# Last sequence of an attention and mixture-of-experts block: residual sums on VectorE, counts added behind the rank, half of the one-hots on GpSimd

## The chip, the cores and the metric

One core of a Trainium2 chip runs one launch of the kernel. The time is device microseconds of that launch, the median of several runs. Instruction times come from one profiled execution, in microseconds from the start of its span. The engines are TensorE (PE, with its weight loads as PEld), VectorE (DVE), ScalarE (ACT), GpSimd (POOL) and SyncE (SP, which here only issues DMAs).

## The reference, cut to what matters

Eight sequences of 256 tokens of width 256 go through an attention layer (16 query heads, 4 key and value heads of 128) and a mixture-of-experts layer (8 experts, two per token, and one shared expert). Both have a normalisation ahead and behind and a residual sum.

```python
x = x + _layernorm(attn(_layernorm(x)))
x = x + _layernorm(ffn(_layernorm(x)))

# ffn, on xf = all 2048 tokens
logits = xf @ gate_w.T
weights, indices = top_k(softmax(logits), 2)      # weights then divided by their sum
out = sum over the 2 experts of weight * (silu(xf @ w_gate[e]) * (xf @ w_up[e])) @ w_down[e]
out = out + sigmoid(xf @ shgate_w) * (silu(xf @ shw_gate) * (xf @ shw_up)) @ shw_down
```

## The kernel before, in words

The 2048 tokens are 16 tiles of 128 tokens, two per sequence: tile i is sequence b = i // 2, half t = i % 2. The last sequence, b = 7, owns tiles 14 and 15.

The order of the work is written out by hand: inside `tc.manual_schedule()` each engine runs its instructions in the order in which the program names them. An engine never passes an instruction that waits, so whatever stands behind it on that engine waits as well. A loop over steps `s` lays the projections, the attention and the routing of several sequences beside each other, each helper with a delay of its own. What does not fit into the loop stands behind it, line by line, for sequence `z = B - 1`.

For each tile the helpers that matter here are, in their order:

- `output` multiplies the attention result by the output weights (L638, PE, into PSUM tile `o`).
- `residual` takes mean and variance of `o` on DVE (`norm_stats`, L258 to L261: `st_o`, `mv_o`), and raises the variance plus epsilon to -0.5 on POOL (L262, `rstd_o`).
- `residual_sum` normalises `o` into `y` on DVE (`norm_apply`, L267) and adds `y` to the residual stream `x_all` on POOL (L653).
- `inner` takes the statistics of `x_all` (again L258 to L262: `st_f`, `mv_f`, `rstd_f`), `inner_rows` normalises into `xf` on DVE (L267) and sends the rows to memory through SP's queue (L663).
- `turn_inner` transposes `xf` on PE (L671, `tf`), ACT copies it into `xfT` (L672).
- `route` computes the router's logits on PE (L678, `r`) and picks the two experts on DVE (L687 to L703); `chosen` and its sum `ch` are one-hots over the 8 experts.
- `rank` counts, on PE, how many earlier tokens took the same expert (L724, L725, `rank`). On DVE, `at` adds an offset (L727), `count` adds this tile's choices to running counts in bf16 (L729, over 64 elements for the first tiles down to 8 for the last), and `pk`, `place`, `pu`, `pr` and `rc` (L733 to L745) turn the rank into a row and a column.
- `mark` writes, for each of the two experts k, three one-hots of 128x128 in bf16 on DVE into one tile `hot` (L756, L757, L761); that tile has one buffer.
- `enter` multiplies the one-hots on PE (L772, `in`): four products per tile, (k = 0, n = 1), (0, 2), (1, 1), (1, 2), each with `hot[k, 0]` as weights. DVE adds the result to `member` (L776).

`fill(n)` puts parts of the shared expert between them: `gus` (L285, PE), `sl` (L297, ACT), `hT` (L298, DVE), `sd` (L305, PE), and a scaled copy (L312, ACT).

Behind the last sequence, `table` sums the counts on PE (L1035, `total`), and a chain on DVE (L1039 to L1060), with PE in between (L1065, L1072), gives the list of tokens of each block. POOL fetches the blocks' rows by indirect DMA (L1136), and 39 blocks follow, each with transposes, two multiplications by the weights of its expert, and a store (L1146 to L1197). At the end the rows are gathered again, combined, normalised and stored.

The order behind the loop, for the last sequence (cut to the calls on the tiles' way):

```python
            for o in range(H, 2 * H):
                output(z, o)
            inner(z, 0)
            inner_rows(z, 0)
            fill(2)
            turn_inner(z, 0)
            residual(z, 1)
            route(z, 0)
            residual_sum(z, 1)
            fill(1)
            rank(z, 0)
            inner(z, 1)
            mark(z, 0)
            inner_rows(z, 1)
```

Of the kernel before, what the change touches and what calls it, by code (L numbers as in the profile page):

```python
# [15 lines left out]
ALU = mybir.AluOpType  # L16
# [3 lines left out]
P = 128  # L20
B, S, HID = 8, 256, 256
# [7 lines left out]
E, TOPK, HE, HS = 8, 2, 176, 352  # L29
# [11 lines left out]
G = len(ENDS)  # L41
# [7 lines left out]
def block_kernel(  # L49
# [18 lines left out]
    nc = tc.nc  # L68
# [10 lines left out]
    x_all = const.tile([P, NTILES, HID], F32, name="x_all")  # L79
# [62 lines left out]
    for j, w in enumerate((wg, wu)):  # L142
# [42 lines left out]
    count = const.tile([P, G, E], BF16, name="count")  # L185
# [14 lines left out]
    iota_p = const.tile([P, P], BF16, name="iota_p")  # L200
    nc.gpsimd.iota(
        iota_p, pattern=[[1, P]], base=0, channel_multiplier=0,
# [49 lines left out]
    stats = {}  # L252
# [12 lines left out]
    def norm_apply(dst, src, name):  # L265
        mean, rstd = stats.pop(name)
        nc.vector.tensor_scalar(dst, src, mean, rstd, ALU.subtract, ALU.mult)  # L267
# [97 lines left out]
    with ExitStack() as actx:  # L365
# [16 lines left out]
        now = {}  # L382
# [266 lines left out]
        def residual_sum(b, t):  # L649
            i = b * NT + t  # L650
            y = xw.tile([P, HID], F32, tag="y", name=f"y_{i}")
            norm_apply(y, now.pop(("o", b, t)), f"o_{i}")
            nc.gpsimd.tensor_tensor(x_all[:, i, :], x_all[:, i, :], y, ALU.add)  # L653

        def inner(b, t):
            i = b * NT + t
# [63 lines left out]
        def rank(b, t):  # L720
            i = b * NT + t
            ch = now.pop(("ch", i))
            ps = ps_tr.tile([P, E], F32, tag="tr", name=f"rank_{i}")
            nc.tensor.matmul(ps, lhsT=before, rhs=ch, start=True, stop=False)  # L724
            nc.tensor.matmul(ps, lhsT=ones, rhs=count[:, G - 1], start=False, stop=True)  # L725
            at = small.tile([P, E], F32, tag="at", name=f"at_{i}")
            nc.vector.tensor_add(at, ps, first)  # L727
            g = sum(i >= end for end in ENDS)
            nc.vector.tensor_add(  # L729
                count[:, g:], count[:, g:], ch[:, None, :].to_broadcast([P, G - g, E])  # L730
            )
            pk = small.tile([P, TOPK, E], F32, tag="pk", name=f"pk_{i}")
            nc.vector.tensor_tensor(  # L733
                out=pk, in0=chosen[:, i], in1=at[:, None, :].to_broadcast([P, TOPK, E]),
                op=ALU.mult,
            )
            nc.vector.tensor_reduce(out=place[:, i], in_=pk, axis=AX.X, op=ALU.add)

            pu = small.tile([P, TOPK], U32, tag="pu", name=f"pu_{i}")
            nc.vector.tensor_copy(pu, place[:, i])  # L740
            pr = small.tile([P, 2, TOPK], U32, tag="pr", name=f"pr_{i}")
            nc.vector.tensor_scalar(pr[:, 0], pu, 7, None, ALU.logical_shift_right)
            nc.vector.tensor_scalar(pr[:, 1], pu, P - 1, None, ALU.bitwise_and)
            rc = small.tile([P, 2, TOPK], F32, tag="rc", name=f"rc_{i}")
            nc.vector.tensor_copy(rc, pr)  # L745
            now["rc", i] = rc

        def mark(b, t):
            i = b * NT + t
            rc = now.pop(("rc", i))  # L750


            hot = xw.tile([P, TOPK, 3, P], BF16, tag="hot", name=f"hot_{i}", bufs=1)
            for k in range(TOPK):
                row, column = rc[:, 0, k : k + 1], rc[:, 1, k : k + 1]
                nc.vector.tensor_scalar(hot[:, k, 0], iota_p, row, None, ALU.is_equal)  # L756
                nc.vector.tensor_scalar(  # L757
                    hot[:, k, 1], iota_p, column, number, ALU.is_equal, ALU.mult
                )
                if i > 0:  # L760
                    nc.vector.tensor_scalar(  # L761
                        hot[:, k, 2], iota_p, column, float(i * P), ALU.is_equal, ALU.mult
                    )
            now["hot", i] = hot
# [62 lines left out]
        with tc.manual_schedule():  # L827
# [68 lines left out]
            for s in range(FIRST, LAST):  # L896
# [26 lines left out]
                ends(s, gates, 8)  # L923
                ends(s, inner_rows, 6)
                ends(s, rank, 9)
                each(deviation, j)
                centre_last(s)
                ends(s, enter, 10)
                each(power, j)
                ends(s, residual_sum, 5)  # L930
                begins(s, prepared, 0, 2)
                begins(s, prepared, 1, 5)
                each(exponential, u)
                outputs(s)
                each(value, u - 2)
                ends(s, mark, 9)
                ends(s, shares, 9)
                if s == B * NS:
# [12 lines left out]

            z = B - 1
            rank(z - 1, 1)
            mark(z - 1, 1)
            shares(z - 1, 1)
            for o in range(sum(OUTPUTS[: LAST - OUT - z * NS]), H):
                output(z, o)
            enter(z - 1, 1)
            residual(z, 0)
            residual_sum(z, 0)  # L960
            for o in range(H, 2 * H):
                output(z, o)
# [4 lines left out]
# [9 lines that stand above are left out]
# [309 lines left out]
    with tc.manual_schedule():  # L1285
# [30 lines left out]
        g, s = G - 3, FULL[G - 3] + 4  # L1316
# [105 lines left out]
```

## Time and profile before

| what | value |
|---|---|
| time before, median of 3 runs | 747.17 us (746.22 to 748.61) |
| profiled execution: its time | 751.43 us |
| profiled execution: span, first to last instruction | 749.7 us |
| granted TensorE clock, mean | 0.987 |
| DVE, ACT, POOL busy, share of the span | 73%, 61%, 53% |
| DVE one-hots L756, L757, L761, mean of one | 0.247, 0.307, 0.249 us |
| DVE normalisation from PSUM L267 `y`, mean of one | 0.535 us |
| POOL sum L653 `x_all`, mean of one | 0.742 us |
| DVE counts L729, shortest and longest | 0.149 and 0.661 us |

The attention loop runs to about 560 us, the end of the last sequence and the table to about 594, the 39 blocks and the final part to the end. A row of the timeline is: start, duration, engine, line, operation, output<-inputs, shapes, count, and in brackets how long the engine sat idle before it and what released it. Successive rows of like instructions are merged, with the count behind x. A group's row has the busy time in all and the mean in ns of one behind the bar, then the idle time before them.

### The profile page before, as it was taken

Reading aid. Unit: us, or ns where it says so; the run is one execution under the profiler, and the core shown is the slowest. Engines: PE = TensorE matmul, PEld = TensorE weight load, DVE = VectorE, ACT = ScalarE, POOL = GpSimd, SP = SyncE. Lnnn points to the kernel's source line nnn. Section 1 sums busy time; section 2 is a strip of 40 time slices with the busy share of each in tenths; the row PEclk is TensorE's granted clock in tenths of the full one; section 3 lists DMA queues with packets and bytes.
Section 4 is the critical chain, followed back from the end, with each engine's and each line's share of the span. In section 5 each row is a group of like instructions: output and inputs, shape, how many; then the busy total and the mean of one; then the engine's idle time right before and its main releaser. Section 6 shows DMA issues by size and latency. Waiting matters only on the chain.

```text
span 749.7 us, 11365 instructions
## 1 busy us (share of the span) xinstructions
PE 718.3 (96%) x3446; PEld 530.0 (71%) x3446; DVE 550.1 (73%) x1494; ACT 458.8 (61%) x1448; POOL 396.5 (53%) x455
## 2 busy tenths in 40 slices
PE   8689999999999999999999999999999999999984
PEld 5356677777777777777777777777887677777664
DVE  5788778789888978887897988679756572455455
ACT  2688877677677767776776777677741333333332
POOL 5667567365555637563664657365212444355534
PEclk9899999999999999999999999999999999999998
DMA  9400000000000000000000000002303133234332
GB/s 317 147 2 1 0 1 8 1 7 1 8 1 7 1 8 8 0 8 1 7 2 8 1 9 7 1 9 80 83 8 92 49 112 107 85 113 126 113 108 77
DMA packets 26916, 32.36 MB, mean 43 GB/s; under 512 B 2980, under 2 KB 23048, under 8 KB 26856
## 3 DMA queue, kind: packets, MB, share of 16 engines
q1 hardware_dynamic: 22752, 21.94, 9.1%
q0 software_dynamic: 3408, 9.31, 4.6%
q8 instruction: 28, 0.46, 0.2%
q10 hardware_dynamic: 696, 0.40, 0.2%
q14 instruction: 32, 0.26, 0.1%
HBM read 22.33 MB, written 9.31 MB: 42 GB/s over the span
## 4 chain that ended last, share of the span: by engine, by line
PE 89%; DVE 4%; ACT 3%; POOL 1%; issue 1%; DMA 0%; DVEq 0%; ACTq 0%; POOLq 0%
PE qkv L411 19%; PE o L638 15%; PE sc L542 10%; PE av L619 10%; PE gu L1166 6%; PE gus L285 5%; PE tp L601 5%; PE py L1191 5%; PE tq L506 4%; PE sd L305 2%; PE xt L1146 1%; PE ht L1181 1%; ACT qn L453 1%; POOL rstds L444 1%; ACT w_qkv L248 1%
## 5 line engine op out<-in xcount | busy, mean ns | idle before, releaser
L411 PE MATMUL qkv<-w_qkv,xnT 128*128 128x512 f32 x384 | 182.8, 601 | 0.0
L479 POOL TENSOR_TENSOR t<-qn,sg_q 128x256 f32<-128x256 f32 x128 | 118.3, 945 | 51.5 <-ACT qn L453 49.9
L444 POOL TENSOR_TENSOR rstds<-ves,nhalf 128x4 f32<-128x4 f32 x80 | 94.0, 1174 | 74.2 <-DVE ves L435 73.7
L638 PE MATMUL o<-wo_sb,oT 128*128 128x256 f32 x512 | 125.8, 385 | 0.0
L453 ACT ACTIVATE qn<-qkv,rstds 128x128 f32<-128x128 f32 x320 | 91.5, 372 | 34.1 <-POOL rstds L444 33.7
L411 PEld LDWEIGHTS qkv<-w_qkv,xnT 128*128 128x128 f32 x384 | 71.5, 193 | 54.2 <-issue 49.7
L570 ACT ACTIVATE ex<-sc,nmx 128x128 f32<-128x128 f32 (+1 forms) x256 | 105.0, 431 | 6.4 <-DVE nmx L559 6.1
L542 PE MATMUL sc<-kT,q 128*128 128x256 f32 (+1 forms) x512 | 99.7, 328 | 2.5 <-DVE q L516 2.5
L619 PE MATMUL av<-pT,v 128*128 128x256 f32 (+1 forms) x320 | 98.6, 422 | 0.6 <-ACT pT L606 0.6
L638 PEld LDWEIGHTS o<-wo_sb,oT 128*128 128x128 f32 x512 | 91.4, 190 | 9.4
L542 PEld LDWEIGHTS sc<-kT,q 128*128 128x128 f32 x512 | 74.7, 191 | 6.0 <-ACT w_qkv L248 2.7
L554 DVE TENSOR_TENSOR sc<-sc,mask 128x256 f32<-128x256 f32 (+1 forms) x96 | 49.2, 513 | 40.4 <-PE sc L542 40.0
L506 PEld LDWEIGHTS tq<-ident,t 128*128 128x128 f32 x320 | 40.0, 143 | 48.1 <-issue 35.1
L606 ACT COPY pT<-tp 128x512 f32<-128x512 f32 x96 | 57.1, 595 | 24.3 <-PE tp L601 24.3
L559 DVE TENSOR_REDUCE nmx<-sc 128x2 f32<-128x512 f32 (+1 forms) x96 | 66.2, 690 | 2.8
L601 PEld LDWEIGHTS tp<-ident,ex 128*128 128x128 f32 x384 | 47.7, 141 | 25.7 <-issue 12.9
L619 PEld LDWEIGHTS av<-pT,v 128*128 128x128 f32 x320 | 59.0, 190 | 9.2 <-ACT pT L606 1.3
L467 DVE TENSOR_TENSOR t<-qn,cg_q 128x512 f32<-128x512 f32 x64 | 57.4, 896 | 8.0 <-ACT qn L453 7.7
L429 ACT ACTIVATE sq<-qkv 128x512 f32<-128x512 f32 x80 | 48.2, 603 | 21.6 <-PE qkv L411 11.8
L435 DVE TENSOR_REDUCE ves<-sq 128x4 f32<-128x516 f32 x80 | 54.6, 682 | 7.2 <-ACT sq L429 7.2
L601 PE MATMUL tp<-ident,ex 128*128 128x128 f32 x384 | 58.5, 274 | 1.4 <-DVE xnT L401 0.7
L590 ACT ACTIVATE ex<-ex,rr 128x256 f32<-128x256 f32 x128 | 58.9, 521 | 0.6 <-DVE rr L578 0.5
(199 smaller groups left out, 1208.2 us busy)
## 6 DMA issues: line engine op xcount, KB each, us to landing
ys<-yb SPq DMA_DIRECT2D x39, 128.0 KB
w_qkv<-in_wqkvT SPq DMA_DIRECT2D x6, 512.0 KB
x_all<-in_x SPq DMA_DIRECT2D x8, 256.0 KB
wo_sb<-in_woT SPq DMA_DIRECT2D x1, 2048.0 KB
xf_rows<-xf SPq DMA_DIRECT2D x16, 128.0 KB
out<-yo SPq DMA_DIRECT2D x14, 128.0 KB
wgu_sb<-in_wg SPq DMA_DIRECT2D x2, 704.0 KB
wgu_sb<-in_wu SPq DMA_DIRECT2D x2, 704.0 KB
```

Source lines behind the costliest of these rows:

```text
L411: nc.tensor.matmul(ps.rearrange("p h d -> p (h d)"), lhsT=seqs[b]["xnT"][t][:, c, :], rhs=w_qkv[g][:, c, :], start=(c == 0), stop=(c == KC ...
L444: nc.gpsimd.tensor_tensor(rstd, now.pop(("ve", b, j)), nhalf, ALU.pow)
L453: nc.scalar.activation(qn[:, h, :], ps[:, h, :], AF.Copy, scale=rstd[:, h : h + 1])
L479: nc.gpsimd.tensor_tensor(t2[:, :, lo : lo + HD], qn[:, :, hi : hi + HD], sg[s][:, t : t + 1, lo : lo + HD].to_broadcast([P, REP, HD]), AL ...
L506: nc.tensor.transpose(tr[:, h, :], t1[:, h, :], ident)
L542: nc.tensor.matmul(sc[:, h, :], lhsT=seqs[b]["qT"][g][:, r0 + h, t * P : (t + 1) * P], rhs=seqs[b]["kT"][:, g, :w], start=True, stop=True,)
L559: nc.vector.tensor_reduce(out=nm, in_=now["sc", b, u], axis=AX.X, op=ALU.max, negate=True)
L570: nc.scalar.activation(ex[:, h, :], sc[:, h, :], AF.Exp, bias=nm[:, h : h + 1], accum_out=rs[:, h : h + 1],)
L590: nc.scalar.activation(ex[:, h, :], ex[:, h, :], AF.Copy, scale=rr[:, h : h + 1])
L601: nc.tensor.transpose(tr[:, c, :], ex[:, h, k * P : (k + 1) * P], ident)
L619: nc.tensor.matmul(now["av"][:, r0 : r0 + nh, :].rearrange("p h q -> p (h q)"), lhsT=seqs[b]["v"][:, k, g * D : (g + 1) * D], rhs=pT[:, k ...
L638: nc.tensor.matmul(now["o", b, t], lhsT=seqs[b]["oT"][h // REP, t][:, h % REP, :], rhs=wo_sb[:, h, :], start=(h == 0), stop=(h == H - 1),)
```

## The change

Three edits, with no change to the order in which the helpers are called. First, in the last sequence, `residual_sum` subtracts the mean on DVE and then multiplies by `rstd` and adds `x_all` in one three-operand DVE instruction; POOL's sum goes. Second, for all tiles, `rank` issues the addition to `count` behind `rc`. Third, in the last sequence, `mark` has the three one-hots of the second expert (k = 1) written by POOL. TensorE, ACT and SP keep their instructions and the order of them.

```diff
         def residual_sum(b, t):
             i = b * NT + t
             y = xw.tile([P, HID], F32, tag="y", name=f"y_{i}")
-            norm_apply(y, now.pop(("o", b, t)), f"o_{i}")
-            nc.gpsimd.tensor_tensor(x_all[:, i, :], x_all[:, i, :], y, ALU.add)
+            o = now.pop(("o", b, t))
+            if b + 1 < B:
+                norm_apply(y, o, f"o_{i}")
+                nc.gpsimd.tensor_tensor(x_all[:, i, :], x_all[:, i, :], y, ALU.add)
+            else:
+                mean, rstd = stats.pop(f"o_{i}")
+                nc.vector.tensor_scalar(y, o, mean, None, ALU.subtract)
+                nc.vector.scalar_tensor_tensor(
+                    x_all[:, i, :], y, rstd, x_all[:, i, :], ALU.mult, ALU.add
+                )
...
             nc.vector.tensor_add(at, ps, first)
             g = sum(i >= end for end in ENDS)
-            nc.vector.tensor_add(
-                count[:, g:], count[:, g:], ch[:, None, :].to_broadcast([P, G - g, E])
-            )
             pk = small.tile([P, TOPK, E], F32, tag="pk", name=f"pk_{i}")
...
             nc.vector.tensor_copy(rc, pr)
             now["rc", i] = rc
+            nc.vector.tensor_add(
+                count[:, g:], count[:, g:], ch[:, None, :].to_broadcast([P, G - g, E])
+            )
...
                 row, column = rc[:, 0, k : k + 1], rc[:, 1, k : k + 1]
-                nc.vector.tensor_scalar(hot[:, k, 0], iota_p, row, None, ALU.is_equal)
-                nc.vector.tensor_scalar(
+
+                engine = nc.gpsimd if b + 1 == B and k == 1 else nc.vector
+                engine.tensor_scalar(hot[:, k, 0], iota_p, row, None, ALU.is_equal)
+                engine.tensor_scalar(
                     hot[:, k, 1], iota_p, column, number, ALU.is_equal, ALU.mult
                 )
                 if i > 0:
-                    nc.vector.tensor_scalar(
+                    engine.tensor_scalar(
                         hot[:, k, 2], iota_p, column, float(i * P), ALU.is_equal, ALU.mult
                     )
```

## The prediction

> **What bounds the kernel.** I read the page first: busy time and the chain that ended last.
>
> ```profile
> PE 718.3 (96%) x3446; PEld 530.0 (71%) x3446; DVE 550.1 (73%) x1494; ACT 458.8 (61%) x1448; POOL 396.5 (53%) x455
> ...
> PE 89%; DVE 4%; ACT 3%; POOL 1%; issue 1%; DMA 0%; DVEq 0%; ACTq 0%; POOLq 0%
> ```
>
> TensorE is busy 96% of the span and 89% of the chain is its own work, so a change on VectorE (DVE) or GpSimd (POOL) matters only where TensorE (PE) waits. The busy time by stretches shows where. In the loop (440 to 540 us) PE is busy 20.00 us in every 20, and the waits of PE between 100 and 545 us list nothing. Between 545 and 568 it is busy 22.40 of 23, between 568 and 594 only 23.24 of 26.00, and in the block stage (594 to 700) again 105.58 of 106. The 2.8 us of gaps after 568 are where the change works, so I read PE's timeline there (start, duration, work, idle time and its releaser).
>
> ```profile
> 573.39 1.46 PE L305 MATMUL sd<-sd_sb,hT 128*128 128x256 f32 x6
> 574.91 0.38 PE L772 MATMUL in<-hot 128*128 128x128 bf16 x2
> 575.45 0.38 PE L772 MATMUL in<-hot 128*128 128x128 bf16 x2 [0.17 <-DVE hot L757]
> 575.94 0.44 PE L671 MATMUL tf<-ident,xf 128*128 128x128 f32 x2
> 576.84 0.61 PE L678 MATMUL r<-gw_sb,xfT 128*128 128x9 f32 x4 [0.46 <-ACT xfT L672]
> 577.30 1.97 PE L285 MATMUL gus<-xfT,sgu_sb 128*128 128x256 f32 x8
> ...
> 582.28 0.54 PE L772 MATMUL in<-hot 128*128 128x128 bf16 x4
> 582.65 0.19 PE L1035 MATMUL total<-count,ones 128*128 128x64 bf16 x1
> 582.68 1.97 PE L285 MATMUL gus<-xfT,sgu_sb 128*128 128x256 f32 x8
> ```
>
> Read the starts. `sd` ends near 574.7, the first pair of `in` starts at 574.91, the second at 575.45 (waiting for one-hots, `hot`), the transposes `tf` of tile 15 at 575.94, `r` at 576.84 after ACT's copy. PE runs in program order, so `tf` cannot pass `in`. For tile 15 the four `in` run without a gap, 107 ns apart (0.54 in all, the last 0.22), so the last starts at 582.60; `total` follows, and the whole table up to the first fetch hangs on it.
>
> The same stretch on DVE:
>
> ```profile
> 572.48 0.15 DVE L727 TENSOR_TENSOR at<-rank,first 128x8 f32<-128x8 f32 x1
> 572.55 0.15 DVE L729 TENSOR_TENSOR count<-count,ch 128x8 bf16<-128x8 bf16 x1
> 572.67 0.18 DVE L733 TENSOR_TENSOR pk<-chosen,at 128x16 f32<-128x16 f32 x1
> ...
> 573.56 0.17 DVE L745 CAST rc<-pr 128x4 f32<-128x4 uint32 x1
> 573.64 0.42 DVE L258 BATCH_NORM_STATS2 st_f<-x_all 128x6 f32<-128x256 f32 x1
> ...
> 575.31 0.25 DVE L761 TENSOR_SCALAR hot<-iota_p,rc 128x128 bf16<-128x128 bf16 x1
> 575.48 0.41 DVE L267 TENSOR_SCALAR xf<-x_all,mv_f,rstd_f 128x256 f32<-128x256 f32 x1
> ```
>
> Two things are to be seen: `pk` starts 0.04 us after the end of `at` (572.48 + 0.15), with `count` inside that gap; and `st_f` of tile 15 starts 0.08 us after `rc` started, because it is only queued behind it. On POOL, tile 15's `rstd_f` runs 574.54 to 575.09 (0.55 us), and `xf` on DVE comes at 575.48 behind the sixth `hot`.
>
> **Edit 1, residual sums of tiles 14 and 15.** Removed: one normalisation on DVE (L267 `y`, 0.535 us) and one sum on POOL (L653, 0.72 us) per tile, with a hand-over. Added on DVE: a subtraction of the same shape from PSUM, taken at 0.535 (L267), and a three-operand instruction, 0.485 (L1282 at the end of the kernel is the same form). Tile 14: the subtraction no longer waits for `rstd_o` and the POOL sum (564.00 to 564.72) goes, so `st_f` moves from 564.76 to about 563.85 and `xf` from 566.25 to about 565.35. But PE runs the 32 output matmuls of tile 15 until 568.44, where `tf` of tile 14 starts; `xf` was done at 566.66, 1.8 us ahead. Gain 0; were that cover absent it would be 0.9 us. Its row DMA leaves 0.9 earlier too, and SP's next entry, the `wd_sb` load at 568.63, starts only as those matmuls end. Tile 15: subtraction at 571.05 as before, sum at 571.61 to 572.09 (`rstd_o` is ready at 571.00). The next DVE instruction, `hT` at 572.14, waits for ACT's `sl`, which ends at 572.11. So the 0.485 us fills an idle stretch of 0.56, and `st_f` still stands behind the rank. Gain 0, slack 0.05; if the sum took as long as POOL's 0.72, +0.2.
>
> **Edit 2, counts behind the rank, all 16 tiles.** Taking `count` from between `at` and `pk` gives nothing: `pk` waits for the end of `at` anyway. Behind `rc` it takes an issue slot (`at` to `count`: 0.07). For tile 15 the follower, `hot`, waits for the end of `rc` (581.15 to 581.36 start to start), so it is free. For tile 14 the follower is the independent `st_f`: +0.07, carried into edit 3. In the loop a `count` takes 0.15 to 0.66 us (0.66 at 177.06, beside POOL's L479), but PE waits for nothing there: 0. `total` reads the counts at 582.65, the new `count` is done by about 581.4.
>
> **Edit 3, three of six one-hots by POOL, tiles 14 and 15.** DVE drops 0.55 us per tile (three starts 0.16, 0.22 and 0.16 apart). `xf` of tile 15 could start at 575.2 in place of 575.48, so `tf` could gain 0.28 if nothing else held it. POOL gains three TENSOR_SCALAR, 128x128 bf16, with a scalar from a column. No row shows one; call its duration D. Nearest rows of POOL:
>
> ```profile
> L444 POOL TENSOR_TENSOR rstds<-ves,nhalf 128x4 f32<-128x4 f32 x80 | 94.0, 1174 | 74.2 <-DVE ves L435 73.7
> ...
> L224 POOL TENSOR_TENSOR so_k<-scratch,gb_all 128x128 f32<-128x128 f32 x2 | 0.9, 457 | 0.0
> ...
> L1247 POOL TENSOR_SCALAR less<-mv_d 128x2 f32<-128x2 f32 x1 | 0.3, 253 | 0.0
> ```
>
> Below: L1247, the same operation on 2 elements, 0.253, so D is hardly less. Above: L444, a power over 4 elements, 1.174. Nearest in size: L224, the same 128x128 with two inputs, 0.457. I take D = 0.457. Consecutive POOL instructions start D - 0.03 apart (the memset at 568.66 lasts 1.80, the next starts at 570.43).
>
> Tile 14: in POOL's program order the three stand behind `rstd_f` of tile 15. That now ends at 574.54 + 0.07 + 0.55 = 575.16, the first one-hot starts at 575.13, and the third ends at 575.07 + 3D. `in` follows 0.05 later (575.40 to 575.45 before) and `tf` 0.11 behind that: 575.23 + 3D against 575.94. Shift: 3D - 0.71 = +0.66.
>
> Tile 15: `rc` ends at 581.32, hand-over 0.08 (`mv_o` 562.71 to `rstd_o` 562.79), third end 581.34 + 3D, last `in` at 581.39 + 3D against 582.60. Shift: 3D - 1.21 = +0.16; it cannot be below 0, as PE is busy until 582.28 and the four then run back to back.
>
> Queued behind them on POOL: after tile 14's only tile 15's; after tile 15's the constants that the table's scan reads at 584.55, which start at 583.03 and would still do so (POOL is free at 582.7). DVE's first one-hot of tile 15 gets a wait for POOL's of tile 14 (one buffer), which end at 576.4, 5 us earlier.
>
> Behind `total` all moves one for one: PE's waits at 586.49 and 590.18 hang on the DVE chain from `total` and on ACT behind PE, and the block stage is PE's.
>
> **Sum.** 0 + 0 + 0.66 + 0.16 = **+0.8 us**. Bounds: D = 0.253 gives 0.05 + 0; D = 1.174 gives 2.81 + 2.31 = 5.1. The profiled execution took 751.43 us (span 749.7 and 1.73 around it), so 752.2 by its measure; it lies 4.26 above the median of the runs shown, 747.17. I carry the difference over unscaled: **748.0 us**.
>
> [...]
>
> [...]
>
> **Rivals.**
> [...]
> - Slower: POOL compares slowly. Place: the last `in` of tiles 14 and 15. Price 6D - 1.92, over 0.3% (2.24 us) from D = 0.69. At the 0.73 of POOL's 128x256 sums (L225) it is 2.5, 749.6; at 1.174 it is 5.1, 752.2. For it: POOL's power costs 0.55, 0.72 and 1.17 us for 1, 2 and 4 elements, so some operations there go by the element. Against: its sums and selects do not.
> - The gain isn't there to take, nor the loss: the stall of 3.81 us at 710.87, whose releaser the profile does not show, swallows the shift. 747.2.
> - Faster by over 2.24 us: the waits that the change can touch on PE (574.7 to 575.94) hold some 0.7, so something outside this reckoning would have to add to it; were all 2.76 us of PE's gaps between 568 and 594 gone, 744.4.
>
> **Numbers.** A measurement of this kernel tells about 0.3% (2.24 us) from no change; the forecast lies inside that. Forecast (D 0.36 to 0.69, +0.4 to +2.2) 0.58; quick POOL 0.10; swallowed 0.07; slow POOL 0.20; faster 0.05. So faster 0.05, same 0.75, slower 0.20. The range: from 746.4 (quick POOL, less the 0.95 by which the lowest run lies under the median, rounded) to 750.7 (D about 0.9); beyond lies the slowest part of the slow rival, about a tenth.
>
> **What would show it.** Edit 1 right: `st_f` of tile 14 about 0.9 earlier relative to its `st_o`, `tf` no earlier relative to the last output matmul. Edit 2: `pk` no earlier behind `at`, `st_f` of tile 15 0.07 later behind `rc`. Edit 3: POOL's one-hots near 0.46; the last `in` of tile 14 released by POOL, some 2.8 us behind the start of `st_f` of tile 15 (before: by DVE, 575.61 against 573.64, 2.0). Wrong: a row for POOL's one-hots under 0.3 or over 0.7, `hT` later behind `sl`, or a PE wait in the loop.

## The result, and the profile after

The changed kernel takes 751.83 us (median of 7 runs, 750.30 to 753.09) against 747.74 us (7 runs, 746.22 to 749.04): a ratio of 1.0048, 95% interval 1.0036 to 1.0061. The medians lie 4.09 us apart; by the ratio it is some 3.6 us (2.7 to 4.6). The forecast was 748.0 us with a range up to 750.7: the time lies outside, and the change is slower where no change was forecast.

The two profiled executions differ by less: 752.52 us against 751.43, spans 750.8 and 749.7. They must not be compared end to end. In the profile of before PE stands still for 3.81 us at 710.87, and its clock is 0.50 from 715.92 to 719.34; the profile after has no such stall there, but starts later (tile 14's `tf` at 570.76 against 568.44). Of these 2.32 us, 2.23 are there at the first scores already (40.28 against 38.05), ahead of all that was changed; from there to tile 14's `tf` it is 530.48 against 530.39 us, so the loop with its moved counts costs some 0.1 at most (530.53 in e1 below). The stall and the clock behind it, in the profile of before:

```profile
714.68 0.44 PE L1146 MATMUL xt<-ident,xb 128*128 128x128 f32 x2 [3.81 <-issue]
```

```profile
716.00:718.00 2.00, 2.00 (x6) 1.35 (x5) 1.02 (x3) 0.32 (x1) 0.00 (x0) 0.50 0.01 4
718.00:720.00 2.00, 2.00 (x8) 1.57 (x7) 1.41 (x5) 0.74 (x2) 0.72 (x1) 0.67 0.19 66
```

(Second fence: the busy time by stretches; the third number from the end of a row is the granted clock of TensorE.) So I measure **the stretch** from the start of tile 14's `tf` to the start of `total`, inside which the change works: 582.65 - 568.44 = 14.21 us before, 589.07 - 570.76 = 18.31 after, 4.10 more.

The page of the changed kernel says nothing yet (first line of its busy times):

```profile
PE 718.1 (96%) x3446; PEld 529.8 (71%) x3446; DVE 550.5 (73%) x1490; ACT 459.9 (61%) x1448; POOL 400.3 (53%) x459
```

PE's timeline of the changed kernel does. Columns as before; these lines answer to the second fence of the prediction.

```profile
579.00 0.22 PE L782 MATMUL in<-hot 128*128 128x128 bf16 x1 [1.31 <-POOL hot L767]
579.80 0.22 PE L782 MATMUL in<-hot 128*128 128x128 bf16 x1 [0.59 <-POOL hot L771]
...
581.17 3.31 PE L285 MATMUL gus<-xfT,sgu_sb 128*128 128x256 f32 x8
...
589.01 0.22 PE L782 MATMUL in<-hot 128*128 128x128 bf16 x1 [0.59 <-POOL hot L771]
589.07 0.19 PE L1045 MATMUL total<-count,ones 128*128 128x64 bf16 x1
```

Three things are to be seen. The third and fourth `in` of tile 14 stand alone, after gaps of 1.31 and 0.59 us that POOL's one-hots end. `gus` behind `r`, the same eight matmuls that took 1.97 us, now take 3.31. And the fourth `in` of tile 15 waits 0.59 us for POOL as well, with `total` behind it. POOL's timeline has the durations that no row of before could give:

```profile
576.95 0.55 POOL L262 TENSOR_TENSOR rstd_f<-mv_f,nhalf 128x1 f32<-128x1 f32 x1 [3.62 <-DVE mv_f L261]
577.49 0.66 POOL L766 TENSOR_SCALAR hot<-iota_p,rc 128x128 bf16<-128x128 bf16 x1
578.14 0.80 POOL L767 TENSOR_SCALAR hot<-iota_p,rc,number 128x128 bf16<-128x128 bf16 x1
579.03 0.72 POOL L771 TENSOR_SCALAR hot<-iota_p,rc 128x128 bf16<-128x128 bf16 x1
```

They take 0.66, 0.80 and 0.72 us, not 0.457, and the third ends 2.26 us after the first began, not 1.31. The busy time by stretches of 2 us shows the other part; the column behind POOL's is the granted clock of TensorE:

```profile
578.00:580.00 2.00, 0.41 (x4) 0.39 (x4) 0.33 (x2) 0.00 (x0) 1.66 (x3) 1.00 0.29 79
580.00:582.00 2.00, 1.54 (x10) 1.22 (x9) 0.86 (x5) 0.37 (x1) 0.00 (x0) 0.91 0.00 0
582.00:584.00 2.00, 2.00 (x6) 1.55 (x6) 0.49 (x5) 0.00 (x0) 0.00 (x0) 0.50 0.03 8
584.00:586.00 2.00, 2.00 (x10) 1.53 (x9) 0.95 (x5) 0.38 (x1) 0.00 (x0) 0.74 0.00 0
```

PE is busy 0.41 us between 578 and 580, and some 2 us after its gaps the clock falls: 0.91, 0.50, 0.74. Of 2 us each, 0.18, 1.00 and 0.52 are missing; at half clock this is (0.18 + 1.00 + 0.52) / 0.5 = 3.4 us. DVE's rows finish the picture:

```profile
573.96 0.48 DVE L659 SCALAR_TENSOR_TENSOR x_all<-y,rstd_o,x_all 128x256 f32<-128x256 f32 x1
574.47 0.42 DVE L298 TENSOR_TENSOR hT<-sl,gus 96x256 f32<-96x256 f32 x1
574.81 0.15 DVE L735 TENSOR_TENSOR at<-rank,first 128x8 f32<-128x8 f32 x1
575.00 0.18 DVE L738 TENSOR_TENSOR pk<-chosen,at 128x16 f32<-128x16 f32 x1
...
575.89 0.17 DVE L750 CAST rc<-pr 128x4 f32<-128x4 uint32 x1
575.97 0.16 DVE L752 TENSOR_TENSOR count<-count,ch 128x8 bf16<-128x8 bf16 x1
576.04 0.42 DVE L258 BATCH_NORM_STATS2 st_f<-x_all 128x6 f32<-128x256 f32 x1
```

`hT` starts at once behind the new sum (573.96 + 0.48) and behind ACT's `sl`, which ends at 574.44, `pk` 0.04 us behind the end of `at` as before without `count` between them, and `st_f` 0.07 us later behind `rc`, all as reckoned.

The 4.10 us are the sum of differences between starts: tile 14's `tf` to tile 15's `tf` 9.10 against 7.50 (+1.60, POOL); from there to `r` 0.85 against 0.90 (-0.05); `r` to `rank` 3.57 against 2.27 (+1.30, the clock); `rank` to the first `in` of tile 15 3.54 against 3.17 (+0.37, the clock in `sd`); to `total` 1.25 against 0.37 (+0.88, POOL).

### The profile page after: what moved, and what is told of

Its sections match the earlier page's. It is cut to its first block, busy times and chain, and to the rows that moved or that the text cites. A ratio compares the mean times of both kernels' runs of the same rounds, so it can differ in the third digit from the quotient of the medians.

```text
span 750.8 us, 11367 instructions
## 1 busy us (share of the span) xinstructions
PE 718.1 (96%) x3446; PEld 529.8 (71%) x3446; DVE 550.5 (73%) x1490; ACT 459.9 (61%) x1448; POOL 400.3 (53%) x459
```

## The experiments

The runs were made on other chips or days, where the kernel before took 746.9 to 755.3 us, so only ratios are compared, and the stretch, which does not depend on the stall at the end. The theory at the start: POOL's slow one-hots open gaps on PE, these make the clock fall, and nothing else costs anything. The rivals: the counts or DVE's sums cost something; the long `gus` has another cause.

| run | stretch, us | lowest clock in it | ratio to before (95%) |
|---|---|---|---|
| before | 14.21 | 1.00 | 1 |
| changed kernel | 18.31 | 0.50 | 1.0048 (1.0036 to 1.0061) |
| e1, edits 1 and 2 | 14.29 | 1.00 | 1.0006 (0.9986 to 1.0025) |
| e2, edit 3 | 19.33 | 0.50 | 1.0034 (1.0020 to 1.0047) |
| e3, PE kept busy | 16.95 | 1.00 | 1.0024 (1.0007 to 1.0041) |
| e4, rows first | 13.47 | 1.00 | 0.9992 (0.9974 to 1.0010) |
| e5, tile 14 | 17.26 | 0.57 | 1.0035 (1.0018 to 1.0052) |
| e6, tile 15 | 15.48 | 1.00 | 1.0028 (1.0008 to 1.0047) |
| e8 and e10, first gap filled | 16.94, 16.95 | 1.00 | one run each |
| e9 and e11, second gap filled | 18.42, 18.41 | 0.50 | one run each |

(The clock is the lowest of the 2 us slices. In e5 the fall to 0.50, from 580.28 to 583.69, fills no slice whole. e7, below, leaves the stretch as it was, 14.22 us, and was run once.)

**e1: edits 1 and 2 alone.**

```diff
-                engine = nc.gpsimd if b + 1 == B and k == 1 else nc.vector
+                engine = nc.vector
```

> Edits 1 and 2 kept, all one-hots back on DVE. Measure: the stretch from the start of tile 14's tf to the start of total, 14.21 us in the profile of before and 18.31 in that of the changed kernel. Theory (all of the loss comes from edit 3): stretch 14.2 to 14.3, time as before, 747.7, ratio 1.000. Rival (the counts in all 16 tiles, or DVE's sums, cost something): stretch 14.5 or more, or PE waits in the loop, and 749 or more.

Stretch 14.29, ratio 1.0006. The two edits cost 0.08 us in the stretch, the issue slot of `count` ahead of `st_f`, and nothing that the times can tell. The rival that blames them falls.

**e2: edit 3 alone**, on the kernel before (the last hunk of the diff).

> Edit 3 alone, on the kernel before. Theory: POOL's one-hots take 0.66 to 0.80 us as in the changed kernel, the granted clock falls to 0.5 for some 3 us after PE's gap, stretch 18.1 to 18.3, ratio 1.005 (751.5). Rival (the edits cost only together, since DVE's sums and counts push the one-hots back): stretch 16 or less, ratio 1.002 or less.

Stretch 19.33, 1.0 us more than with all edits; ratio 1.0034, the interval up to 1.0047. Edit 3 carries the loss by itself, and the rival that needs all edits together falls. The stretch is longer than expected because the clock was low for twice as long, 0.63, 0.50, 0.50 and 0.66 in the slices from 578 to 586: (0.74 + 1.00 + 1.00 + 0.68) / 0.5 = 6.8 us at half clock. This profiled execution was the slowest of e2's twelve runs (760.68 us, median 756.02), so it need not be typical.

**e3: the changed kernel, with PE kept busy.**

```diff
+                if b + 1 == B and k == 1:
+                    if n == 1:
+                        spare = ps_o.tile([P, P], F32, tag="o", name=f"spare_{i}")
+                    for _ in range((12, 6)[n - 1] if t == 0 else (0, 5)[n - 1]):
+                        nc.tensor.transpose(spare, ident, ident)
                 nc.tensor.matmul(
                     ps, lhsT=hot[:, k, 0], rhs=hot[:, k, n],
```

> The changed kernel, with idle transposes of the identity into a spare PSUM bank where PE waits for POOL's one-hots (12 and 6 in tile 14, 5 in tile 15); nothing of the computation is changed. Theory (PE's gap of 2 us makes the granted clock fall to 0.5 afterwards, and this costs 1.6 us): clock 1.00 all through, gus behind r 1.97 us in place of 3.31, stretch 16.7, time 1.6 us below the changed kernel, about 750.2. Rival (the long gus has another cause, or the clock falls anyway): stretch 18.3, 751.8. If the transposes overrun the wait, stretch up to 0.3 longer than either.

PE's timeline in it:

```profile
577.45 1.48 PE L786 MATMUL spare<-ident 128*128 128x128 f32 x12
578.92 0.22 PE L787 MATMUL in<-hot 128*128 128x128 bf16 x1
...
581.10 1.97 PE L285 MATMUL gus<-xfT,sgu_sb 128*128 128x256 f32 x8
```

And the busy time by stretches, where the changed kernel has a clock of 0.50:

```profile
582.00:584.00 2.00, 2.00 (x12) 1.67 (x12) 0.93 (x6) 0.38 (x1) 0.00 (x0) 1.00 0.00 0
```

The useless transposes fill the gaps, POOL's one-hots take as long as in the changed kernel (0.66, 0.80 and 0.71), the clock stays at 1.00, and `gus` is back at 1.97 us. The stretch is 16.95, expected 16.7. So more work on PE makes the stretch 1.36 us shorter, and the clock is shown to be the cause of the long `gus`: the rival falls. The times of whole runs do not tell it: the interval of 1.0024 overlaps that of the changed kernel's 1.0048.

**e5 and e6: POOL's one-hots in one tile alone.**

```diff
-                engine = nc.gpsimd if b + 1 == B and k == 1 else nc.vector
+                engine = nc.gpsimd if b + 1 == B and k == 1 and t == 0 else nc.vector    # e5; t == 1 in e6
```

> The changed kernel with POOL's one-hots in tile 14 alone. Theory (POOL's 2.2 us behind the power open two gaps on PE, and the clock falls after them): tile 14's tf to tile 15's tf 9.1 us (7.5 before), the clock falls to 0.5 about 2 us after the gaps, stretch from tile 14's tf to total 17.4 to 18.4, time between 1.003 and 1.005 of before. Rival (the clock's fall needs tile 15's gap too): stretch 15.8, clock 1.00, 1.002.

> The changed kernel with POOL's one-hots in tile 15 alone. Theory: the last in of tile 15 waits for POOL's third one-hot, total 0.9 us later, no fall of the clock: stretch 15.1, 1.001 of before. Rival (tile 15's wait is hidden by the work behind, or part of tile 14's delay): stretch 14.3, 1.000.

Tile 14 alone: tile 14's `tf` to tile 15's 9.08 us, the clock falls for 3.4 us, stretch 17.26 (17.4 to 18.4 was expected), that is 2.97 over e1. Tile 15 alone: 15.48 (15.1 was expected), 1.19 over e1, clock 1.00. PE there:

```profile
585.21 0.22 PE L782 MATMUL in<-hot 128*128 128x128 bf16 x1 [0.43 <-POOL hot L767]
586.01 0.22 PE L782 MATMUL in<-hot 128*128 128x128 bf16 x1 [0.59 <-POOL hot L771]
```

The two add up to 4.16 against the 4.02 by which the changed kernel exceeds e1. In the changed kernel tile 15's part is smaller, 0.88, because PE at half clock comes to `in` later (the 0.37 us above), while POOL's chain goes on. Without a fall of the clock the sum is e1 plus 1.51 (tile 14, 9.08 against 7.57 in e1) plus 1.19, 16.99, and e3 has 16.95. The theory on both holds.

**e8 to e11: which gap brings the clock down.** The transposes of e3 in tile 14's first gap alone (e8, and the same kernel again as e10), or 1 in the first and 6 in the second (e9, again as e11).

> The changed kernel, 12 idle transposes on PE in tile 14's first gap (1.47 us) alone; the second (0.74 us) and tile 15's stay open. Theory A (the clock falls on a long gap, over some 1 us): clock 1.00, stretch 16.7. Theory B (it falls on any gaps of this size): clock 0.5 for 3 us, stretch 18.

> The changed kernel, 6 idle transposes in tile 14's second gap alone, and 1 in the first, whose remaining 1.3 us stay open. Theory A (a gap of over 1 us is enough): the clock falls to 0.5, stretch 18. Theory B (it takes both, 2.2 us in some 2.5): clock 1.00, stretch 16.7.

> The same kernel as the one with tile 14's first gap filled, for another look at the clock. Theory A (PE's gap of 1.2 to 1.3 us makes the clock fall, and it is filled here): clock 1.00, stretch 16.9. Theory W (the clock is set by stretches of 3.4 us that run on by themselves, so it depends on where the gaps fall in them): the clock may fall in one look and not in another, here less often than with the first gap open.

> The same kernel as the one with tile 14's second gap filled and 1.2 us of the first open, for another look at the clock. Theory A: the clock falls again, for 3.4 us, stretch 18.4. Theory W: the clock may stay at 1.00 in this look (stretch 16.8), as it did in the gap of 2.46 us before 38.05 us in the profile of before; if it falls, then for a multiple of 3.4 us.

With only the gap of 0.59 us open the clock stays at 1.00 behind tile 14 in both runs, with one of 1.2 us open it falls in both, for 3.4 us. Over these profiles: in the five in which tile 14's gap of 1.2 to 1.3 us is open (the changed kernel, e2, e5, e9, e11) the clock falls to 0.50 behind it, in seven others (before, e1, e3, e4, e6, e8, e10) it stays at 1.00 in the stretch. PE in e9:

```profile
576.80 0.22 PE L787 MATMUL in<-hot 128*128 128x128 bf16 x1 [1.20 <-POOL hot L767]
...
578.98 3.44 PE L285 MATMUL gus<-xfT,sgu_sb 128*128 128x256 f32 x8
```

That is theory A for this place. But as a rule on the length of a gap it does not hold. All kernels have the same gap of some 2.5 us early on, where PE waits for the first scores. In twelve of the thirteen profiles, where it is 2.41 to 2.52 us long (2.46, up to 38.05, in before), the clock stayed at 1.00 behind it. In e8, where it is 2.57 us and ends at 38.26, the busy time by stretches is this (granted clock behind POOL's column):

```profile
38.00:40.00 2.00, 1.74 (x5) 1.20 (x6) 1.64 (x4) 2.00 (x10) 1.99 (x3) 0.79 0.02 4
40.00:42.00 2.00, 2.00 (x4) 0.87 (x3) 1.34 (x4) 1.69 (x8) 1.63 (x3) 0.50 0.03 8
42.00:44.00 2.00, 2.00 (x12) 1.35 (x12) 1.89 (x6) 1.18 (x4) 2.00 (x3) 0.86 0.00 0
```

A fall of 3.4 us: 0.42, 1.00 and 0.28 missing of 2 us each, at half clock. So gaps of up to 2.52 us passed here where 1.2 us did not there: something besides the length decides, as theory W has it. But e9 and e11 ran nearly in the same position (their clock fell in the same slices from 8 us on), so their agreement does not tell.

The stretches of theory W are in the traces. In slices of 0.2 us the clock of before falls to 0.50 at 9.37, 23.02 and 715.92 us and is back at 1.00 at 12.78, 29.85 and 719.34 (a fourth fall, at 743.23, lasts to the end of the span). These three last 3.41, 6.83 and 3.41 us, and from the first to the second are 13.65 us, 4 times 3.413, to the third 706.55, 207 times 3.413. The changes that the slices of the other twelve profiles show lie whole multiples of 3.413 us apart too: in the changed kernel the falls at 15.03 and 581.65 are 166 of them apart, in e2 those at 25.56 and 578.52 are 162. So the changes of the clock seen here lie on a grid of 3.413 us that is still the same some 700 us later (before). The place on this grid alone does not bring the clock down: e2 and e10 lie nearly alike (the third `in` of tile 14 starts 0.43 us ahead of a point of the grid in e2, and 0.27 in e10, counted on from its fall at 24.68), and only e2, with the gap open, falls there. What brings the clock down is not shown, and the share of time in which PE is busy between two points of the grid does not tell: e8 from 35.77 to 39.18, with 0.92 us busy, and e9 from 575.91 to 579.32, with 2.05, end in a fall, and e2 from 35.80 to 39.21, with 1.53, does not.

**e7: what a TENSOR_SCALAR on POOL costs.** The kernel before, with nine more in a stretch where POOL idles (two of them shown):

```diff
             enter(z - 1, 1)
+            pool(bforms[:, :P], iota_p, col, None, ALU.is_equal)
...
+            pool(bforms[:, :P], iota_p, 5.0, None, ALU.mult)
             residual(z, 0)
```

> The kernel before, with nine more TENSOR_SCALAR on POOL into tiles that nothing reads, in a stretch in which POOL idles (551 to 562 us); nothing of the computation is changed. In order: the three one-hot forms on 128x128 bf16 (column; column and column; column and constant), then a constant in place of the column, then a multiplication in place of the comparison, then the column form on 64 and on 2 elements, then the column form and the multiplication on 128x128 f32. Theory (the time is that of a loop over the elements, 0.25 us fixed and 3 ns per element): 0.66, 0.80, 0.72, then 0.65, 0.65, 0.45, 0.26, and f32 as bf16. Rival 1 (the column scalar costs): the fourth about 0.4. Rival 2 (the comparison costs): the fifth about 0.4. Rival 3 (bf16 costs): the two in f32 about 0.4. Rival 4 (a fixed cost): 0.6 on 2 elements too.

Four of the nine, POOL's timeline: the column form, a constant in its place, a multiplication in place of the comparison, the column form on 2 elements.

```profile
553.09 0.66 POOL L964 TENSOR_SCALAR bforms<-iota_p,number 128x128 bf16<-128x128 bf16 x1
...
555.55 0.53 POOL L967 TENSOR_SCALAR bforms<-iota_p 128x128 bf16<-128x128 bf16 x1
556.16 0.53 POOL L968 TENSOR_SCALAR bforms<-iota_p 128x128 bf16<-128x128 bf16 x1
...
557.34 0.29 POOL L970 TENSOR_SCALAR bforms<-iota_p,number 128x2 bf16<-128x2 bf16 x1
```

The three one-hot forms took 0.66, 0.80 and 0.72 us, as in the changed kernel, so they are not slow because DVE works beside them: here DVE has one row between 553.09 and 558.5, `xf` up to 553.60. The theory's fourth and fifth number were wrong (0.53, not 0.65), the others near: 64 elements 0.445, 2 elements 0.29, and in f32 0.61 with a column and 0.53 with a constant. So here a comparison cost what a multiplication did, 0.53 us (rival 2 falls), a column in place of a constant cost 0.13 us (rival 1 has half of its price), bf16 at most 0.05 (rival 3 falls), and there is a part of up to 0.29 that 2 elements paid too (no 0.6, rival 4 falls) and, worked out from 2, 64 and 128 elements, 2.5 to 3.3 ns per element in the column form. Between most of them POOL also idles some 0.1 us (0.66 long, 0.76 from start to start), in the changed kernel between the second and the third, but not between the first two (0.66 long, 0.65).

**e4: a version with neither.** e1 with tile 15's rows ahead of tile 14's one-hots, on DVE and on PE:

```diff
-            rank(z, 0)
             inner(z, 1)
-            mark(z, 0)
+            rank(z, 0)
             inner_rows(z, 1)
+            mark(z, 0)
             fill(2)
-            enter(z, 0)
             turn_inner(z, 1)
             route(z, 1)
+            enter(z, 0)
             fill(1)
```

> Edits 1 and 2, all one-hots on DVE, and the order behind the loop changed: statistics of tile 15 ahead of tile 14's rank, its rows ahead of tile 14's one-hots, its transposes and router logits on PE ahead of tile 14's in. Theory (since edit 1 has x_all of tile 15 ready 1.5 us before st_f starts, the wait is one of DVE's order): r of tile 15 about 1 us earlier, stretch 13.2, time 1.0 us below before, 746.7, ratio 0.999. Rival (the 0.75 us of statistics ahead of the rank come back as late one-hots): stretch 14.2 or more, ratio 1.000.

PE in it:

```profile
577.97 0.41 PE L679 MATMUL tf<-ident,xf 128*128 128x128 f32 x2 [0.16 <-DVE xf L267]
578.84 0.61 PE L686 MATMUL r<-gw_sb,xfT 128*128 128x9 f32 x4 [0.46 <-ACT xfT L680]
579.31 0.38 PE L782 MATMUL in<-hot 128*128 128x128 bf16 x4
```

Tile 15's `r` starts 7.45 us after tile 14's `tf` (8.40 before), and the four `in` fill the time between `r` and `gus` without a gap. The stretch is 13.47, 0.74 under before, where 1.0 was expected. The ratio, 0.9992, has an interval that holds both 1 and the 0.999 expected: it beats the changed kernel, and whether it beats the one before its time does not tell.

## Why the prediction was wrong

- **What bounds the kernel** held: no wait of PE appears in the loop, and all of the change that the profiles show lies behind tile 14's `tf`.
- **Edit 1** held: `st_f` of tile 14 starts 2.01 us behind its `st_o` (2.88 before, 0.87 gained), hidden behind the output matmuls on PE; tile 15 gains nothing, and e1 shows no loss. The subtraction took 0.47, not 0.535.
- **Edit 2** held: +0.07 at `st_f`, 0.08 in e1's stretch.
- **Edit 3, "I take D = 0.457"**: this step failed first. The mean of the three is 0.73, and the step that had them start D - 0.03 apart failed with it, since they start 0.65 and 0.89 apart. The third ends 2.26 us after the first starts, not 1.31: 0.95 more per tile. With that the two shifts become 0.66 + 0.95 = 1.61 (measured 1.60) and 0.16 + 0.95 = 1.11 (1.19 in e6). So the term of edit 3, put at 0.8 us, measures 2.8 without the clock. Two of the three rows are over the 0.7 that was named as a sign of being wrong. The mechanism was right, and the size belonged to the rival that had 0.20: its line for 0.73 said 2.5 us. Its reason, that POOL compares slowly, was not right: in e7 a multiplication takes the same 0.53. The 0.36 from which the forecast's chance counts D is shown by no run: POOL's one-hots took 0.66 to 0.80 here, and 0.53 with a constant in e7; its selects, named beside the slow rival, took 0.28 (before, L162, 128x128 bf16). L224, nearest in size, has the wrong form, and L1247, with the right one, was taken as an end only: it is near the 0.29 that 2 elements take in e7, to which 128 elements had to be added.
- **What no step had**: the gaps are not paid once, and the sum has no term for what follows them. The clock falls behind them, which cost 1.36 us in the stretch (18.31 against e3's 16.95). This put the time outside the range: 747.17 + 1.60 + 1.19 = 750.0 lies inside it, and 1.36 more, 751.3, does not. That it may happen could have been read in before: behind the stall at 710.87 the slices from 716 to 720 have a clock of 0.50 and 0.67. That it must could not: behind the gaps of 2.46 us (up to 38.05) and 1.59 us (up to 46.58) the same trace has 1.00. The slow rival was priced without it, 749.6 where it should have been near 751.
- **"Behind `total` all moves one for one"**: nearly. From tile 14's `tf` to the first `xt` the difference is 26.90 - 23.11 = 3.79, since PE's waits at `pickp` and `sd` shrank from 0.54 and 0.67 to 0.35 and 0.56 us. The stall at 710.87 swallows nothing: the medians lie 4.09 us apart, the stretches 4.10, a match that is closer than runs spread over some 3 us can promise. It does not hang on the change either: e8 has one of 4.65 us, up to 719.06, and e10, the same kernel, has none.

## What to carry to other kernels

Before work moves to an engine that stands idle, price it by a row of the same form, and where there is none, forecast with the whole range and not with the nearest neighbour alone (the middle of the range here, 0.71, is near the 0.73 measured, but by luck); then look at what stands ahead of it on that engine, here a power that it had to queue behind (in tile 14 `rc` was done at 576.06 us, the power ran from 576.95, and the first one-hot started behind it at 577.49). Price a new gap on TensorE twice: its length, and the slower clock that may follow it (here 1.36 us), as the trace of before shows, with 0.50 behind its stall of 3.81 us. A wait that comes from the order in which one engine was given its work can be removed by another order: e4, with edits 1 and 2 in it and no one-hot moved, took 0.74 us out of the stretch. Whether the order alone, without these two edits, would do so was not run.

## What was not expected of the hardware

- Useless transposes in a gap of PE made the stretch 1.36 us shorter (18.31 to 16.95).
- The changes of the clock that were seen lie on a grid of 3.413 us. In the stretch its falls lasted 3.4 us or, in e2, 6.8, and began 1.7 us (e2) to 4.3 us (e5) after the start of tile 14's first gap.
- POOL spent 2.5 to 3.3 ns per element on a one-input comparison in bf16 with a column (e7): 128 elements took 0.53 us with a constant and 0.66 to 0.80 with columns, where DVE took 0.25 to 0.31 for the same one-hots.
